# Residual updates in batches of rows through SBUF, and the weighting of the quantile sums moved behind the next step's products

## The chip, the core and the metric

The kernel runs on one core of a Trainium2 chip. Its engines each work through a queue of their own, in order: TensorE (PE in the profile, with PEld for its weight loads), VectorE (DVE), ScalarE (ACT), GpSimd (POOL), and SyncE (SP), whose queue issues the transfers. Semaphores connect them. The metric is the time of one execution on the device, in microseconds. The kernel before takes 12865.49 us, the median of three runs (12863.24, 12865.49 and 12865.96).

## What is computed

The input is `x` (16 graphs of 1024 nodes with 64 features) and a dense 0/1 adjacency matrix per graph. Four layers follow each other, each with a residual:

```
h = relu(layernorm(x)); x = x + L0(h, adj)   # thinned adjacency, weighted quantiles, two-layer MLP
h = relu(layernorm(x)); x = x + L1(h, adj)   # ((adj + I) @ h) / rowsum, NaN replaced by 0
h = relu(layernorm(x)); x = x + L2(h, adj)   # attention of 8 heads, adjacency as a bias
h = relu(layernorm(x)); x = x + L3(h, adj)   # adj @ (h @ W) + b
```

Layer 0 is the unusual one. For each node and each feature it takes the quartiles 0.25, 0.5 and 0.75 over the values of the node's neighbours, each interpolated between two ranks, and sums them with weights 0.25, 0.5 and 0.25. So there are NQ = 6 rank queries (two for each of three quantiles).

## The kernel before

The kernel is written in a framework with tile pools. A pool has a tag and a number of buffers; a new tile of a tag takes a buffer that an older tile has left, and waits if there is none. The framework orders the instructions of each engine when the kernel is built, by their place in the program, by what they depend on and by free buffers. The resulting order of each engine's queue is fixed in the program that runs.

Two streams are woven together. The first is layer 0 (`picks`): 1536 steps, one for each graph (16), group of 8 features (8), half of the nodes (2) and query q (6). Step n runs `compare(n)`: DVE makes `le` (is the count below the rank), `wa` and `wb` (its products with two tables); PE folds `wb` and `wa` into the PSUM tile `prep` and `le` into `val`; ACT copies them out into `wi` and `vs`. In the same step come `bits(n-1)` (DVE `bit`, PE `pz`) and `value(n-2)` (DVE multiplies `vs` by a test of `pz`). After the sixth query `value` also sums the six `vs` with PE into the PSUM tile `agg`, DVE multiplies it by the weights `coef` into `w`, PE reduces `w` into `acc`, ACT copies that out, and SP writes it to a tile `z`. The `vs` tiles have a tag of their own with 8 buffers. The tables for the next six steps, the ranking of the next pair of graphs and the thinning of the next adjacency are made in the background of these steps.

The second stream is layers 1 to 3 of the graph before (`rest`). Each of its pieces yields a cost (0.3 for a block of 128 rows in layers 1 and 3, 1.0 for a block of rows and a pair of heads in layer 2), and every step of `picks` gives it 0.42 to spend. A graph has 96 steps, so 40.32 to spend, and `rest` costs 40.5. After the last step the remainder runs by itself, with more buffers (`alone`): that is what is left of graph 14 and all of graph 15.

In that stream the result of each block of rows ends in PSUM, and DVE adds it to the residual `xr` of shape [128, 8, 64] block by block:

- layer 1: row sums `rc` come out of an ACT pass over the adjacency; `weighted` makes `po` (128 x 64) in PSUM; DVE adds `h`, multiplies by 1/`rc`, tests for NaN, copies the good values into a tile that POOL has set to zero, and adds that to `xr`;
- layer 2: for each of 4 pairs of heads and 8 blocks of rows: PE scores `sp`, DVE adds the adjacency and finds the maximum (`s`, `nm`), ACT makes the exponentials with their sums, PE transposes them (`pcols`, ACT copy `eT`) and multiplies by `v` (`ao`), ACT copies (`aoT`), PE projects (`pp`, two heads of 64 columns); DVE takes the reciprocals `rs` of the sums and adds both heads to `xr` with two fused instructions;
- layer 3: `weighted` again, and DVE adds `po` to `xr`.

The tiles in PSUM share these tags: two buffers each for `pa` (`prep`, `val`, `pz`), `pc` (`px`), `pb` (`pcols`, `ao`, `pp`, `po`, `agg`, `acc` and most others) and one of twice the width for `sp`.

Of the kernel before, what the change touches and what calls it, by code (L numbers as in the profile page):

```python
# [8 lines left out]
F32 = mybir.dt.float32  # L9
BF = mybir.dt.bfloat16  # L10
# [24 lines left out]
R_TOP, R_ONE, R_MID = 32, 33, 34  # L35
# [3 lines left out]
def tile_preln_adj_stack(  # L39
# [91 lines left out]
    ident = const.tile([P, P], BF, name="ident")  # L131
    nc.vector.tensor_copy(ident, identf)
    identh = const.tile([P, P], HP, name="identh")
    nc.vector.tensor_copy(identh, identf)
# [129 lines left out]
    nc.vector.tensor_tensor(ident2, identf[:, :D], identf[:, D:], OP.add)  # L264
    ones = const.tile([P, P], BF, name="ones")
# [14 lines left out]
    shifts = const.tile([P, 6], F32, name="shifts")  # L280
# [13 lines left out]
    nc.vector.memset(shifts[:, 5:6], 1.0)  # L294

# [16 lines left out]
    sel_k = const.tile([P, NQ, P], BF, name="sel_k")  # L312
    for q in range(NQ):
        at_row(sel_q[:, q, :], ((q, -KHI), (R_TOP, ones_top * KHI), (R_MID, KHI)))
        at_row(sel_k[:, q, :], ((q, 2.0), (R_MID, -2.0), (R_ONE, 2.0)))
# [5 lines left out]
    at_row(q_add, [(q, 6.0) for q in range(1, NQ, 2)] + [(R_TOP, 8.0), (R_ONE, 8.0), (R_MID, 3.0)])  # L321
# [212 lines left out]
    def ranks(V):  # L534
# [58 lines left out]
        for n in range(len(steps) - 1, -1, -1):  # L593
# [17 lines left out]
            nc.tensor.transpose(pt[:, j, :], R[:, j * P : (j + 1) * P], identh) for j in range(C)  # L611
# [7 lines left out]
    def positions(valid):  # L619

        m1 = sb.tile([P, N], I16, tag="m1", bufs=1, name="m1")
        for t in range(NH):
            pm = pa("pm")
            adjoining(
                nc.tensor.matmul(pm, ones, valid[t][:, j, :], start=j == 0, stop=j == C - 1)
                for j in range(C)  # L630
            )
            nc.vector.tensor_scalar(m1[:, t * 512 : (t + 1) * 512], pm, -1.0, None, op0=OP.add)
            if t < NH - 1:
                yield None
        n6 = a2("n6", (P, N), I16)
        nc.vector.tensor_scalar(n6, m1, q_tau, q_add, op0=OP.mult, op1=OP.add)
        nc.vector.tensor_scalar(n6, n6, 3, None, op0=OP.logical_shift_right)
        kq = sb.tile([P, N], HP, tag="kq", bufs=2, name="kq")
        nc.scalar.copy(kq, n6)
        yield kq  # L640
        krow = []
        for q in range(NQ):

            krow.append(sb.tile([P, N], I16, tag="krow", bufs=NQ, name="krow"))
            for t in range(NH):
                hs = slice(t * 512, (t + 1) * 512)
                pk = pb("pkr")
                nc.tensor.matmul(pk, sel_k[:, q, :], kq[:, hs], start=True, stop=True)
                nc.scalar.copy(krow[q][:, hs], pk)
            if q < NQ - 1:  # L650
                yield None
        yield krow
        nr = a2("nr", (P, N), I16)
        nc.vector.tensor_scalar(nr, m1, r_tau, None, op0=OP.mult)
        nc.vector.tensor_scalar(nr, nr, 3, None, op0=OP.bitwise_and)
        coef = sb.tile([P, N], BF, tag="coef", bufs=1, name="coef")
        nc.vector.tensor_scalar(coef, nr, w_frac, w_one, op0=OP.mult, op1=OP.add)
        yield coef
# [112 lines left out]
    def picks():  # L771
# [8 lines left out]
        weights, tables, state, vs_of, els = {}, {}, {}, {}, {}  # L780
# [24 lines left out]
        def compare(n):  # L805
# [9 lines left out]
            nc.vector.tensor_tensor(wb, le, c1, OP.mult)  # L815
# [24 lines left out]
            vs = sb.tile([P, 512], F32, tag="v", bufs=8, name="vs")  # L840
# [15 lines left out]
        def value(n):  # L856
            b, g, t, q = steps[n]
            el = els[b]
            pz, vs = state.pop(n)
            nc.vector.scalar_tensor_tensor(vs, pz, 97.0, vs, op0=OP.is_equal, op1=OP.mult)  # L860
            vs_of[q] = vs
            if q < NQ - 1:
                return
            agg = pb("agg")
            adjoining(
                nc.tensor.matmul(  # L866
                    agg[32 * (q_ % 4) : 32 * (q_ % 4) + 32, :], sel_t[:, q_ // 4, :], vs_of[q_],
                    start=q_ < 4, stop=q_ > 1, tile_position=(0, 32 * (q_ % 4)),
                    skip_group_check=True,
                )  # L870
                for q_ in range(NQ)
            )
            hs = slice(t * 512, (t + 1) * 512)
            w = a2("w")
            nc.vector.tensor_tensor(w, agg, el.coef[:, hs], OP.mult)
            acc = pb("acc", (8, 512))
            nc.tensor.matmul(acc, sel_c, w, start=True, stop=True)
            nc.scalar.copy(w[:8, :], acc)
            nc.sync.dma_start(el.z[t * D + 8 * g : t * D + 8 * g + 8, t, :], w[:8, :])
# [15 lines left out]
        for n in range(last + 2):  # L895
# [21 lines left out]
            if 0 <= n - 2:  # L917
                value(n - 2)
                if (n - 1) % per == 0:
                    leave(els.pop(steps[n - 2][0]))  # L920
                    for _ in stages:
                        pass
# [151 lines left out]
    def layer1(b, xr, adjT_d):  # L1074
        h = b2_("h1", (P, C, D))
        norm_relu(xr, h, b2_)
        yield 0.5
        for i in range(C):
            ad = adj_rows(b, i)

            rc = small("rc1", [P, 1], bufs=2)
            act(ad, ad, AF.Copy, accum_out=rc)
            nc.vector.tensor_scalar(rc, rc, 1.0, None, op0=OP.add)
            nc.vector.reciprocal(rc, rc)
            aT = chunk_cols(ad, "aT1")
            nc.sync.dma_start(adjT_d[i], aT)
            po = weighted(aT, h)
            o = small("o1", [P, D], bufs=2)
            nc.vector.tensor_tensor(o, po, h[:, i, :], OP.add)
            nc.vector.tensor_scalar(o, o, rc, None, op0=OP.mult)  # L1090

            ok = small("ok1", [P, D], I32, bufs=2)
            nc.vector.tensor_tensor(ok, o, o, OP.is_equal)
            z = small("z1", [P, D], bufs=1)
            nc.gpsimd.memset(z, 0.0)
            nc.vector.copy_predicated(z, ok, o)
            nc.vector.tensor_tensor(xr[:, i, :], xr[:, i, :], z, OP.add)
            yield 0.3

    def layer2(b, xr):  # L1100
# [17 lines left out]
        HW = H * D  # L1118
        for pr in range(H // 2):

# [29 lines left out]
            for i in range(C):  # L1150
                ad = adj_rows(b, i)
                act(ad, ad, AF.Copy, scale=gm[:, i, 1:2])
                sums = small("sums", [P, 2])
# [3 lines left out]
                for t in range(NH):  # L1157
# [13 lines left out]
                    for e in range(2):  # L1171
# [6 lines left out]
                        nms[e] = nm  # L1178
                for e in range(2):
                    act(ss[e], ss[e], AF.Exp, bias=nms[e], scale=-1.0, accum_out=sums[:, e : e + 1])  # L1180
# [9 lines left out]
                rs = small("rs", [P, 2])  # L1190
                nc.vector.reciprocal(rs, sums)
# [4 lines left out]
                for e in range(2):  # L1196
                    nc.vector.scalar_tensor_tensor(
                        xr[:, i, :], pp[:, e, :], rs[:, e : e + 1], xr[:, i, :], op0=OP.mult, op1=OP.add
                    )
                yield 1.0  # L1200

    def layer3(b, xr, adjT_d):
# [10 lines left out]
        yield 0.5  # L1213
        for i in range(C):
            aT = sb.tile([P, C, P], F32, tag="bt", bufs=2, name="aT3")
            nc.sync.dma_start(aT, adjT_d[i])
            po = weighted(aT, hid)
            nc.vector.tensor_tensor(xr[:, i, :], xr[:, i, :], po, OP.add)
            yield 0.3
        nc.sync.dma_start(out[b].rearrange("(c p) d -> p c d", p=P), xr)  # L1220
# [60 lines left out]
```

## Time and profile before

The profiled execution took 12858.39 us; its span from the first to the last instruction is 12856.6 us, so 1.8 us lie around it.

| engine | busy us | share of the span | instructions |
|---|---|---|---|
| PE | 11601.9 | 90% | 86209 |
| DVE | 11662.2 | 91% | 21644 |
| ACT | 9453.7 | 74% | 16250 |
| POOL | 24.5 | 0% | 138 |

The mean granted clock of TensorE is 0.986. Three stages can be told apart in time. The first step of `picks` starts at 350 us; before that DVE ranks the first pair of graphs (PE is busy for 45 of these 350 us). The steps run until the last `le` at 12458 us. From about 12484 us to the end the last graph's layers run alone. A share of busy time is a mean over these stages. "Idle before" in a group of instructions is the time for which the engine did nothing just ahead of them, and the arrow names what it waited for.

### The profile page before, as it was taken

The numbers are of one execution on the slowest core, as the hardware profiler recorded it, in microseconds if no ns is written. First come the engines' busy times: TensorE is split into PE (matmuls) and PEld (weight loads), VectorE is DVE, ScalarE is ACT, GpSimd is POOL, SyncE is SP. The second block draws the span as 40 slices with busy tenths as digits, with TensorE's granted clock in tenths as the row PEclk, the third lists the DMA queues.
The fourth block names the chain that finished last, engine by engine and source line by source line (L and its number), as shares of the span: only waits on it lengthen the run. The fifth ranks groups of instructions, "written<-read, shape, count | busy, mean of one in ns | idle before, by whom it ended". The sixth has DMA issues, their size and how long they took to land. (4 is left out here: it accounts for less than half of the span.)

```text
span 12856.6 us, 221392 instructions
## 1 busy us (share of the span) xinstructions
PE 11601.9 (90%) x86209; PEld 5418.0 (42%) x86209; DVE 11662.2 (91%) x21644; ACT 9453.7 (74%) x16250; POOL 24.5 (0%) x138
## 2 busy tenths in 40 slices
PE   0789999999999998999999999999999999999998
PEld 0224444444444444444444444444444444444445
DVE  8999999999998999989899998999989999887873
ACT  0557777777777787777777777777777777787766
POOL 0000000000000000000000000000000000000000
PEclk9999999999999999999999999999999999999999
DMA  3012121221212122121221212122121221212012
GB/s 104 29 40 70 53 90 53 83 66 58 81 53 87 55 64 77 56 87 56 69 67 60 86 54 84 53 62 83 50 87 54 72 73 56 93 31 66 29 61 67
DMA packets 503198, 841.36 MB, mean 65 GB/s; under 512 B 238720, under 2 KB 273664, under 8 KB 502144
## 3 DMA queue, kind: packets, MB, share of 16 engines
q1 hardware_dynamic: 502144, 827.20, 20.7%
q8 instruction: 675, 11.06, 0.4%
q14 instruction: 379, 3.10, 0.1%
HBM read 616.27 MB, written 206.57 MB: 64 GB/s over the span
## 5 line engine op out<-in xcount | busy, mean ns | idle before, releaser
L813 DVE TENSOR_TENSOR wa<-le,c 128x2048 f16<-128x2048 f16 x1536 | 1879.9, 1224 | 161.7 <-PE prep L832 136.4
L727 PE MATMUL px<-valid,cw 128*128 128x512 fp8e4 x8192 | 1979.6, 382 | 0.0
L811 DVE TENSOR_TENSOR le<-cum,krow 128x2048 f16<-128x2048 int16 x1536 | 1878.3, 1223 | 17.3 <-PE val L832 15.2
L815 DVE TENSOR_TENSOR wb<-le,c 128x2048 f16<-128x2048 f16 x1536 | 1878.6, 1223 | 1.2 <-PE prep L832 1.2
L398 ACT ACTIVATE c<-px,shifts 128x512 f16<-128x512 f32 x2048 | 1414.9, 696 | 381.6 <-PE px L748 197.7
L398 ACT ACTIVATE wi<-prep,shifts 128x512 f32<-128x512 f32 x1536 | 1066.6, 694 | 491.2 <-PE prep L832 343.8
L398 ACT ACTIVATE s<-s,nm 128x1024 f32<-128x1024 f32 x1024 | 1167.6, 1142 | 243.7 <-DVE nm L1174 235.9
L727 PEld LDWEIGHTS <-cw 128*128 128x128 f16 x8192 | 801.1, 98 | 1081.1 <-issue 193.4
L1165 PE MATMUL sp<-kT,qT 64*128 64x512 f32 x4096 | 1163.1, 642 | 90.8 <-DVE nm L1174 86.5
L398 ACT ACTIVATE high<-px,shifts 128x512 f16<-128x512 f32 x1024 | 713.8, 697 | 688.1 <-PE px L727 686.8
L451 PE MATMUL pcols<-identf,s 128*128 128x128 f32 x8192 | 1132.8, 281 | 91.6 <-ACT s L398 40.9
L860 DVE SCALAR_TENSOR_TENSOR vs<-pz,vs 128x512 f32<-128x512 f32 x1536 | 1059.5, 690 | 113.6 <-PE pz L853 105.9
L451 PEld LDWEIGHTS pcols<-identf,s 128*128 128x128 f32 x8192 | 889.6, 141 | 597.2 <-ACT eT L454 270.2
L832 PE MATMUL val<-le,tab 128*32 128x512 f16 x12288 | 1112.7, 385 | 20.4 <-DVE vs L860 11.9
L454 ACT COPY eT<-pcols 128x512 f32<-128x512 f32 x2048 | 1105.6, 598 | 17.7 <-PE pcols L451 16.0
L1184 PE MATMUL ao<-eT,v 128*64 128x128 f32 x16384 | 1075.0, 276 | 41.2 <-ACT eT L454 37.9
L398 ACT ACTIVATE vs<-val 128x512 f32<-128x512 f32 x1536 | 926.4, 603 | 185.7 <-PE val L832 108.5
L1184 PEld LDWEIGHTS ao<-eT,v 128*64 128x64 f32 x16384 | 904.3, 137 | 326.5 <-ACT eT L454 249.3
L1174 DVE CUSTOM_DVE_ANT_0 s<-sp,ad,nm 128x512 f32<-128x512 f32 x1024 | 732.5, 751 | 75.7 <-PE sp L1165 75.0
L398 ACT ACTIVATE low<-px,shifts 128x512 f16<-128x512 f32 x1024 | 706.8, 696 | 81.5 <-PE px L739 80.1
L1174 DVE CUSTOM_DVE_ANT_0 s<-sp,ad 128x512 f32<-128x512 f32 x1024 | 686.2, 691 | 85.2 <-PE sp L1165 57.9
L832 PE MATMUL prep<-wb,sel_w 128*32 128x512 f16 x6144 | 639.8, 393 | 134.3 <-DVE wb L815 130.9
(263 smaller groups left out, 19090.6 us busy)
## 6 DMA issues: line engine op xcount, KB each, us to landing
ad<-in_adj_dram SPq DMA_DIRECT2D x768, 512.0 KB
adjT_d<-aT SPq DMA_DIRECT2D x128, 512.0 KB
aT<-adjT_d SPq DMA_DIRECT2D x128, 512.0 KB
md<-sm SPq DMA_DIRECT2D x216, 256.0 KB
sb<-md SPq DMA_DIRECT2D x216, 256.0 KB
rem_d<-rem SPq DMA_DIRECT2D x128, 256.0 KB
left_d<-nb SPq DMA_DIRECT2D x128, 256.0 KB
lr<-left_d SPq DMA_DIRECT2D x256, 128.0 KB
```

The source lines that it names most:

```text
L398: nc.scalar.activation(out_, in_, func, **kw)
L451: nc.tensor.transpose(pt[:, c, :], ad[:, (4 * s + c) * P : (4 * s + c + 1) * P], identf)
L454: nc.scalar.copy(aT[:, 4 * s : 4 * s + 4, :], pt)
L727: yield nc.tensor.matmul(px[pp], w[:, j, :], valid[:, j, :], start=False, stop=j == C - 1, skip_group_check=True,)
L811: nc.vector.tensor_tensor(le, cum, bc(el.krow[q][:, None, hs], [P, 4, 512]), OP.is_lt)
L813: nc.vector.tensor_tensor(wa, le, c0, OP.mult)
L815: nc.vector.tensor_tensor(wb, le, c1, OP.mult)
L832: yield nc.tensor.matmul(dst[32 * pp : 32 * pp + 32, :], w[pp], r[pp], start=i == 2, stop=i in (1, 3), tile_position=(0, 32 * pp), skip_gr ...
L860: nc.vector.scalar_tensor_tensor(vs, pz, 97.0, vs, op0=OP.is_equal, op1=OP.mult)
L1165: nc.tensor.matmul(sps[e], qT[e * D : (e + 1) * D, i * P : (i + 1) * P], kT[e * D : (e + 1) * D, hs], start=True, stop=True,)
L1174: nc.vector.tensor_tensor_reduce(ss[e][:, hs], sps[e], ad[:, hs], -1.0, 3.0e38 if t == 0 else nms[e], op0=OP.add, op1=OP.min, accum_out=nm,)
L1184: nc.tensor.matmul(ao[e * D : (e + 1) * D, :], v[:, j, e * D : (e + 1) * D], eTs[e][:, j, :], start=j == 0, stop=j == C - 1, tile_position ...
```

## The change

Layers 1 to 3 no longer update `xr` block by block from PSUM. ACT copies each block's result into an SBUF tile (`o1` and `o3` of 128 x 512, one buffer; `att` of 128 x 4 x 2 x 64, one buffer). DVE then works on the whole tile: in layers 1 and 3 once per graph, in layer 2 once for every four blocks of rows, and there only after the maxima of the block that follows. The NaN test becomes `not_equal`, with the zero copied over the bad values from a constant, so that POOL has no more tiles to clear. Layer 1 gets an additional `yield 0.2`.

In `picks` the part of `value` behind `agg` becomes a function `weigh`, which is called in the next step's `compare` and put behind its `wb` on DVE.

Three edits make room in SBUF: one identity matrix instead of two, the matrices `sel_k` left out (ACT makes `krow` from the `sel_q` product, with a scale and a bias), and 7 buffers instead of 8 for `vs`.

```diff
-    ident = const.tile([P, P], BF, name="ident")
+    ident = const.tile([P, P], HP, name="ident")
...
-    identh = const.tile([P, P], HP, name="identh")
-    nc.vector.tensor_copy(identh, identf)
...
+    none = const.tile([P, 1], F32, name="none")
+    nc.vector.memset(none, 0.0)
...
-        at_row(sel_k[:, q, :], ((q, 2.0), (R_MID, -2.0), (R_ONE, 2.0)))
...
-                nc.tensor.matmul(pk, sel_k[:, q, :], kq[:, hs], start=True, stop=True)
-                nc.scalar.copy(krow[q][:, hs], pk)
+                nc.tensor.matmul(pk, sel_q[:, q, :], kq[:, hs], start=True, stop=True)
+                act(krow[q][:, hs], pk, AF.Identity, scale=-2.0 / KHI, bias=shifts[:, 6:7])
...
-            nc.vector.tensor_tensor(wb, le, c1, OP.mult)
+            last = nc.vector.tensor_tensor(wb, le, c1, OP.mult)
+            while owing:
+                owing.pop()(last)
...
-            vs = sb.tile([P, 512], F32, tag="v", bufs=8, name="vs")
+            vs = sb.tile([P, 512], F32, tag="v", bufs=7, name="vs")
...
-            hs = slice(t * 512, (t + 1) * 512)
-            w = a2("w")
-            nc.vector.tensor_tensor(w, agg, el.coef[:, hs], OP.mult)
-            acc = pb("acc", (8, 512))
-            nc.tensor.matmul(acc, sel_c, w, start=True, stop=True)
-            nc.scalar.copy(w[:8, :], acc)
-            nc.sync.dma_start(el.z[t * D + 8 * g : t * D + 8 * g + 8, t, :], w[:8, :])
+            def weigh(behind):
+                hs = slice(t * 512, (t + 1) * 512)
+                w = a2("w")
+                with tc.issue_after(behind.ins) if behind else ExitStack():
+                    nc.vector.tensor_tensor(w, agg, el.coef[:, hs], OP.mult)
+                acc = pb("acc", (8, 512))
+                nc.tensor.matmul(acc, sel_c, w, start=True, stop=True)
+                nc.scalar.copy(w[:8, :], acc)
+                nc.sync.dma_start(el.z[t * D + 8 * g : t * D + 8 * g + 8, t, :], w[:8, :])
+
+            owing.append(weigh)
...
+        o = sb.tile([P, C, D], F32, tag="po", bufs=1, name="o1")
+        rc = small("rc1", [P, C], bufs=2)
         for i in range(C):
             ad = adj_rows(b, i)
-
-            rc = small("rc1", [P, 1], bufs=2)
-            act(ad, ad, AF.Copy, accum_out=rc)
-            nc.vector.tensor_scalar(rc, rc, 1.0, None, op0=OP.add)
-            nc.vector.reciprocal(rc, rc)
+            act(ad, ad, AF.Copy, accum_out=rc[:, i : i + 1])
             aT = chunk_cols(ad, "aT1")
             nc.sync.dma_start(adjT_d[i], aT)
-            po = weighted(aT, h)
-            o = small("o1", [P, D], bufs=2)
-            nc.vector.tensor_tensor(o, po, h[:, i, :], OP.add)
-            nc.vector.tensor_scalar(o, o, rc, None, op0=OP.mult)
-
-            ok = small("ok1", [P, D], I32, bufs=2)
-            nc.vector.tensor_tensor(ok, o, o, OP.is_equal)
-            z = small("z1", [P, D], bufs=1)
-            nc.gpsimd.memset(z, 0.0)
-            nc.vector.copy_predicated(z, ok, o)
-            nc.vector.tensor_tensor(xr[:, i, :], xr[:, i, :], z, OP.add)
+            nc.scalar.copy(o[:, i, :], weighted(aT, h))
             yield 0.3
+        nc.vector.tensor_scalar(rc, rc, 1.0, None, op0=OP.add)
+        nc.vector.reciprocal(rc, rc)
+        nc.vector.tensor_tensor(o, o, h, OP.add)
+        nc.vector.tensor_tensor(o, o, bc(rc[:, :, None], [P, C, D]), OP.mult)
+        bad = b2_("bad", (P, C, D), I32)
+        nc.vector.tensor_tensor(bad, o, o, OP.not_equal)
+        nc.vector.copy_predicated(o, bad, bc(none[:, :, None], [P, C, D]))
+        nc.vector.tensor_tensor(xr, xr, o, OP.add)
+        yield 0.2
...
+            def residual(i, att, sums):
+                rows = xr[:, i : i + C // 2, :]
+                rs = small("rs", [P, C // 2, 2], bufs=1)
+                nc.vector.reciprocal(rs, sums)
+                nc.vector.tensor_tensor(
+                    att, att, bc(rs[:, :, :, None], [P, C // 2, 2, D]), OP.mult
+                )
+                for e in range(2):
+                    nc.vector.tensor_tensor(rows, rows, att[:, :, e, :], OP.add)
...
+                while late:
+                    residual(*late.pop())
                 for e in range(2):
-                    act(ss[e], ss[e], AF.Exp, bias=nms[e], scale=-1.0, accum_out=sums[:, e : e + 1])
+                    act(ss[e], ss[e], AF.Exp, bias=nms[e], scale=-1.0, accum_out=sums[:, i % (C // 2), e : e + 1])
...
-                rs = small("rs", [P, 2])
-                nc.vector.reciprocal(rs, sums)
...
-                for e in range(2):
-                    nc.vector.scalar_tensor_tensor(
-                        xr[:, i, :], pp[:, e, :], rs[:, e : e + 1], xr[:, i, :], op0=OP.mult, op1=OP.add
-                    )
+                nc.scalar.copy(att[:, i % (C // 2)], pp)
+                if (i + 1) % (C // 2) == 0:
+                    late.append((i + 1 - C // 2, att, sums))
                 yield 1.0
+        residual(*late.pop())
...
+        o = sb.tile([P, C, D], F32, tag="po", bufs=1, name="o3")
         for i in range(C):
...
-            po = weighted(aT, hid)
-            nc.vector.tensor_tensor(xr[:, i, :], xr[:, i, :], po, OP.add)
+            nc.scalar.copy(o[:, i, :], weighted(aT, hid))
             yield 0.3
+        nc.vector.tensor_tensor(xr, xr, o, OP.add)
```

More of the change, by code (lines that the diff above doesn't have):

```diff
@@ L34 @@
 FIRST = 127.0
-R_TOP, R_ONE, R_MID = 32, 33, 34
+R_TOP, R_MID = 32, 34
 @with_exitstack
@@ L279, in tile_preln_adj_stack @@
     nc.vector.tensor_scalar(off[:, 1:2], bkt, 0.0, None, op0=OP.is_equal)
-    shifts = const.tile([P, 6], F32, name="shifts")
+    shifts = const.tile([P, 7], F32, name="shifts")
     nc.vector.tensor_scalar(
@@ L294, in tile_preln_adj_stack @@
     nc.vector.memset(shifts[:, 5:6], 1.0)
+    nc.vector.memset(shifts[:, 6:7], 2.0 * (160.0 - FIRST) + 2.0)
     def at_row(dst, terms):
@@ L311, in tile_preln_adj_stack @@
     sel_q = const.tile([P, NQ, P], BF, name="sel_q")
-    sel_k = const.tile([P, NQ, P], BF, name="sel_k")
     for q in range(NQ):
         at_row(sel_q[:, q, :], ((q, -KHI), (R_TOP, ones_top * KHI), (R_MID, KHI)))
-        at_row(sel_k[:, q, :], ((q, 2.0), (R_MID, -2.0), (R_ONE, 2.0)))
     mid_w = const.tile([P, P], BF, name="mid_w")
@@ L320, in tile_preln_adj_stack @@
     q_add = const.tile([P, 1], F32, name="q_add")
-    at_row(q_add, [(q, 6.0) for q in range(1, NQ, 2)] + [(R_TOP, 8.0), (R_ONE, 8.0), (R_MID, 3.0)])
+    at_row(q_add, [(q, 6.0) for q in range(1, NQ, 2)] + [(R_TOP, 8.0), (R_MID, 3.0)])
     r_tau = const.tile([P, 1], F32, name="r_tau")
@@ L610, in ranks @@
         adjoining(
-            nc.tensor.transpose(pt[:, j, :], R[:, j * P : (j + 1) * P], identh) for j in range(C)
+            nc.tensor.transpose(pt[:, j, :], R[:, j * P : (j + 1) * P], ident) for j in range(C)
         )
@@ L779, in picks @@
         ]
-        weights, tables, state, vs_of, els = {}, {}, {}, {}, {}
+        weights, tables, state, vs_of, els, owing = {}, {}, {}, {}, {}, []
         def make(el, g, t):
@@ L919, in picks @@
                 if (n - 1) % per == 0:
+                    while owing:
+                        owing.pop()(None)
                     leave(els.pop(steps[n - 2][0]))
@@ L1118, in layer2 @@
         HW = H * D
+        late = []
         for pr in range(H // 2):
+            def residual(i, att, sums):
[7 more added lines that the diff above has]
+                    nc.vector.tensor_tensor(rows, rows, att[:, :, e, :], OP.add)
             if alone and pr % 2:
@@ L1150, in layer2 @@
             for i in range(C):
+                if i % (C // 2) == 0:
+                    att = sb.tile([P, C // 2, 2, D], F32, tag="att", bufs=1, name="att")
+                    sums = small("sums", [P, C // 2, 2], bufs=2)
                 ad = adj_rows(b, i)
                 act(ad, ad, AF.Copy, scale=gm[:, i, 1:2])
-                sums = small("sums", [P, 2])
                 eTs = []
```

## The prediction

> **What bounds the kernel now.** The first view is the page's busy times: PE 90% and DVE 91% of the span, ACT 74%, POOL nothing. Two engines are nearly full, so neither share alone says what a microsecond on DVE is worth. For that I read the chain of waits.
>
> ```profile
> PE 21%; DVE 19%; ACT 7%; issue 2%; DMA 0%; SPq 0%; ACTq 0%; DVEq 0%
> DVE wa L813 3%; PE px L727 3%; DVE wb L815 3%; DVE le L811 3%; DVE s L1174 3%; PE ao L1184 2%; ACT s L398 2%; PE pcols L451 2%; PE sp L1165 1%; DVE vs L860 1%; PE prep L832 1%; PE val L832 1%; PE agg L866 1%; DVE bit L847 1%; ACT eT L454 1%
> ```
>
> The chain adds up to only half of the span because its earliest piece is at 6518.65 us. Over that second half DVE has 0.19 x 12856.6 = 2443 us on the chain, of 5565 us busy by the windows view of this stretch: 0.44. ACT has 7%, 900 of 4791 us: 0.19. So I count a microsecond of work taken off DVE as 0.44 on the end, and one put on ACT as 0.19. That is a rate for small shifts, not a law.
>
> Then the groups that the change touches, with the idle time ahead of them:
>
> ```profile
> L1197 DVE SCALAR_TENSOR_TENSOR xr<-pp,rs,xr 128x64 f32<-128x64 f32 x1024 | 291.0, 284 | 137.4 <-PE pp L1195 132.9
> L875 DVE TENSOR_TENSOR w<-agg,coef 128x512 f32<-128x512 f32 x256 | 177.0, 691 | 100.7 <-PE agg L866 67.4 <-PE pz L852 31.9
> L1191 DVE RECIPROCAL rs<-sums 128x2 f32<-128x2 f32 x512 | 84.7, 165 | 84.4 <-ACT s L398 80.5
> L1089 DVE TENSOR_TENSOR o<-po,h 128x64 f32<-128x64 f32 x128 | 28.6, 223 | 66.2 <-PE po L1071 64.8
> L1218 DVE TENSOR_TENSOR xr<-xr,po 128x64 f32<-128x64 f32 x128 | 27.9, 219 | 90.6 <-PE po L1071 90.1
> L1083 DVE TENSOR_SCALAR rc<-rc 128x1 f32<-128x1 f32 x128 | 18.7, 150 | 33.3 <-ACT ad L398 33.1
> ```
>
> The reader is to see that DVE, the busiest engine, stands for 512.6 us ahead of these short instructions, out of about 1194 us that it is idle at all. Each is the end of a chain through PE and ACT, sits in DVE's queue at a fixed place, and holds up `le`, `wa` and `wb` behind it.
>
> Last, the timeline of DVE, because durations overlap:
>
> ```profile
> 12451.09 0.16 DVE L1191 RECIPROCAL rs<-sums 128x2 f32<-128x2 f32 x1
> 12451.17 1.21 DVE L811 TENSOR_TENSOR le<-cum,krow 128x2048 f16<-128x2048 int16 x1
> 12452.29 0.69 DVE L860 SCALAR_TENSOR_TENSOR vs<-pz,vs 128x512 f32<-128x512 f32 x1
> 12452.89 0.68 DVE L1174 CUSTOM_DVE_ANT_0 s<-sp,ad 128x512 f32<-128x512 f32 x1
> ...
> 12456.77 0.29 DVE L1197 SCALAR_TENSOR_TENSOR xr<-pp,rs,xr 128x64 f32<-128x64 f32 x1
> 12456.96 0.69 DVE L860 SCALAR_TENSOR_TENSOR vs<-pz,vs 128x512 f32<-128x512 f32 x1
> ```
>
> The next instruction starts 0.08 to 0.09 us before the last one ends. An instruction so takes its duration less 0.09: the reciprocal 0.08, an `xr` update 0.19, a 512-wide one 0.60.
>
> **The change, part by part.** The sum is made against 12858.39 us.
>
> *DVE's work.* Layer 2 removes 512 x (0.08 + 2 x 0.19) = 236 us. It adds 128 batches: a reciprocal of 8 columns (0.20 by L424, so 0.11), a 512-wide product (0.60) and two 256-wide sums. No row has that width; between 0.13 (64 wide, 0.22 less 0.09) and 0.60 (512 wide) a line through the element counts gives 0.33, and 128 x 1.37 = 175 us (124 to 244 at the ends). Layer 1 removes seven instructions a block, 0.15, 0.16, 0.22, 0.25, 0.22, 0.23 and 0.22 us, less 7 x 0.09: 128 x 0.82 = 105 us; it adds per graph two small ones (0.17) and five 512-wide ones: 16 x 3.17 = 51 us. `not_equal` and the predicated copy are not in the trace at this width; at 64 they cost what an addition does, so I take an addition's row. Layer 3 goes from 128 x 0.13 = 17 to 16 x 0.60 = 10 us. Together -61 - 54 - 7 = -122 us, times 0.44: **-54** (ends -106 to +1, from the two widths and no effect). `w` keeps its 256 x 0.69.
>
> *DVE's waits.* The new instructions read SBUF tiles that ACT filled, in layer 2 a whole block of rows later, so the 512.6 us have no cause at these places. At the rate of 0.44 they are 226 us. Not all comes back: DVE arrives earlier at `wa`, which already waits 161.7 us, 136.4 of it for PE's `prep`. I take two thirds, **-150** (ends 0 and -226). The weakest share is `w`: in the built order of the changed program it stands on average 15.7 DVE instructions behind the last `vs` product of its group, before 15.9. Only its short distances are gone (the second tenth goes from 7 to 9.4). Its `acc`, ACT copy and SP transfer go with it; SP already stands 1191.8 us at that transfer for ACT, and the adjacency loads queued behind it run three buffers ahead (ACT waits 33.7 us for them at L398's `ad` in layer 2), so I cost that at nothing; without that cover it would be these 34 us.
>
> *ACT's work.* 512 copies of `pp`, like L1193 (same shape, 0.291): 149 us. 256 of `po`, between L398's accumulator read of one column (0.209) and L1069 (128 wide, 0.267): 0.24, 61 us (54 to 68). `krow` takes a bias, so L398's 0.696 in place of L649's 0.596: 192 x 0.10 = 19 us. The built order has 42 table loads in place of 34; in the timeline each pushes its neighbours 1.31 us apart: 10 us. Together 239 us x 0.19 = **+45** (ends 0 and +239).
>
> The Trainium skill, page "ScalarE: Activation LUTs", section "What ACT_TABLE_LOAD costs", gives about 2.66 us for a switch with its drain, where the trace shows 1.31; by the page the eight loads would be an estimated 21 us, and the term +47. Its section "Rules for kernel authors" speaks against the change: additions and the like belong on VectorE, which is faster per element. What that rule leaves out is which queue is full, and the chain's shares are about that.
>
> *ACT's waits.* Each new copy stands right behind a PE product of its own block, as `aoT` does. Those wait 148.5 us (L1193, 512 of them) and 158.7 us (L1069, 256), 307 us together. The new ones wait for one short product (`pp`, 0.48 us) where `aoT` waits for 16 or 32, so I take half, 154 x 0.19 = **+29** (ends 0 and +307). Queued behind are `wi`, `vs` and the `px` copies, which PE waits for.
>
> *Seven `vs` buffers.* With eight, the copy `vs<-val` of a group's third step takes the buffer that the group's `agg` has to read first; with seven it is the second step. The trace has this wait already: "ACT vs L398 <- PE agg L866: 67.3, 51". In the built order this copy now stands 7.8 ACT instructions behind its `wi`, before 1.6, so `val` keeps one of two `pa` banks meanwhile. Pairing `agg` with `val` step by step through the timeline, I find `agg` ending after the third step's `val` in 92 of 255 groups; holding `prep` until then would push it by 548 us in all. The ends are 0 and 548 x 0.44 = 241; since a freed bank before `agg` lets other work run, I take half of the nearest row, **+34**.
>
> *The rest.* 19 pairs of constant instructions and six matrices leave the start, at about 0.13 us each pair beside other work: **-3** (0 to -8). `rest` now costs 40.7 a graph against 40.32: over 15 graphs the overhang grows from 2.7 to 5.7, three more units run behind the last step. A block alone takes (12810 - 12567) / 31 = 7.8 us, and 3 x 7.8 = 23 are added where as much PE work leaves the steps; less overlap, and three longer ends of layers, make **+10** (0 to +30). POOL's 128 clears hid under DVE: nothing.
>
> Sum: -54 - 150 + 45 + 29 + 34 - 3 + 10 = -89, so 12769 us on the profiled execution. The median stands 7.1 us above it: **12776 us**, -0.7%.
>
> **The rivals.**
>
> *No change.* PE is the bound and the freed waits return at `wa<-prep`: of the 150 only 61 stay, and the sum is 0: 12865 us. For it: PE is busy for 365 to 380 us of most stretches of 400. Against it: 130.9 us of PE's own idle time ahead of `prep<-wb` and 88.6 ahead of `pz<-bit` wait for DVE.
>
> *Slower by the bank.* The late `vs` copy keeps `val`'s bank, `prep` and `pz` share the other, and DVE starves at `wa` and `vs`. At its full 241 in place of 34 the sum is +118: 12984 us. It decides from 34 + 89 = 123 us on, that is 123 / 0.44 / 92 = 3.0 us in each late group, out of at most 6. For it: the two banks and the order; against it: the 67.3 us that the same wait costs now.
>
> *Slower by ACT.* If ACT's copies weigh as much as DVE's work did, 0.44 x (239 + 154) = 173 replaces 74: sum +10, 12875 us; with all 307 of waits +77, 12943 us.
>
> **How the numbers follow.** A difference counts from 0.2%, 26 us, about what a measurement of this kernel tells from none. Forecast 0.56, no change 0.14, the bank 0.20, ACT 0.10. The forecast's own range is 12585 (DVE work at its end, waits at theirs, no new waits: -106 - 226 + 45 - 3 + 10 = -280) to 12840. Across the cases, 12560 to 12990: lower than the forecast's end because the 0.44 may be too small where DVE alone is full, and up to the bank's 12984. Faster 0.57, within 0.2% 0.12, slower 0.31.
>
> **What would show it.** Right: DVE's idle time ahead of the new batches near zero, DVE busy down by about 120 us, PE's share up, more steps per 1000 us in layers 1 and 3. Wrong: `vs<-val` waiting for `agg` far above 67 us; idle ahead of `wa` and `vs L860` grown by what left the updates; ACT's `att` copy waiting for `pp` as long as DVE did. The prediction fails if the built order, which no row of before prices, makes other products late.

## The result, and the profile after

The changed kernel takes 12743.22 us, the median of four runs (12737.83 to 12749.5), against 12864.36 for the kernel before (12861.37 to 12865.96). The ratio is 0.9904 with a 95% interval of 0.9892 to 0.9917: 121 us less. The forecast was 89 less, with the same sign. The profiled execution took 12739.76 us with a mean granted clock of 0.987.

The page's busy times and its chain of waits, for the kernel after:

```profile
PE 11508.7 (90%) x86209; PEld 5414.4 (43%) x86209; DVE 11510.5 (90%) x19675; ACT 9625.0 (76%) x17026; POOL 1.4 (0%) x10
...
DVE 29%; PE 28%; ACT 10%; issue 5%; DMA 1%; SPq 0%; DVEq 0%; ACTq 0%
```

DVE works 151.7 us less and ACT 171.3 us more, where 122 and 239 were forecast. The shares of busy time are nearly what they were, and the chain covers another part of the span than the chain of the kernel before, so neither tells where the time came from. The windows view, cut at the three stages, tells more. Its columns are the stretch, its length, and for each engine the busy time with the number of instructions. First the kernel before, then the kernel after:

```profile
0.00:350.00 350.00, 44.89 (x187) 19.63 (x188) 287.56 (x842) 50.76 (x77) 1.50 (x11) 0.98 0.32 95
350.00:12459.00 12109.00, 11216.00 (x83389) 5167.22 (x83389) 11219.03 (x20311) 9165.43 (x15741) 21.95 (x120) 0.99 0.21 64
12459.00:12856.00 397.00, 341.03 (x2639) 231.11 (x2635) 155.60 (x493) 237.47 (x433) 1.06 (x7) 0.89 0.27 84
```

```profile
0.00:347.00 347.00, 45.21 (x187) 19.77 (x188) 284.29 (x793) 52.33 (x78) 1.35 (x10) 0.98 0.31 96
347.00:12308.00 11961.00, 11098.85 (x83194) 5145.97 (x83193) 11080.40 (x18491) 9306.43 (x16422) 0.00 (x0) 0.99 0.20 65
12308.00:12738.00 430.00, 364.66 (x2830) 248.65 (x2828) 145.85 (x393) 266.22 (x528) 0.00 (x0) 0.89 0.25 82
```

The start is 3 us shorter, the steps 148, and what runs alone at the end is 33 longer. In the steps DVE (the third pair of numbers) is busy for 139 us less. It is idle there for 12109 - 11219 = 890 us before and 11961 - 11080 = 881 after. So by DVE's own account the steps lost work and kept nearly all of their idle time. PE's account (the first pair) adds up as well: with the same 86209 instructions in the whole kernel it is busy for 117 us less in the steps (the ends of its products are modelled). Such an account says what fits, not what caused it.

The groups view of the kernel after, with the instructions that took the place of the updates, and `w`:

```profile
L1130 DVE TENSOR_TENSOR att<-att,rs 128x512 f32<-128x512 f32 x128 | 88.2, 689 | 78.2 <-ACT att L1213 78.2
L1237 DVE TENSOR_TENSOR xr<-xr,o 128x512 f32<-128x512 f32 x16 | 11.0, 690 | 60.9 <-ACT o L1235 60.9
L1129 DVE RECIPROCAL rs<-sums 128x8 f32<-128x8 f32 x128 | 25.8, 202 | 29.7 <-ACT s L397 29.3
L1096 DVE TENSOR_TENSOR o<-o,h 128x512 f32<-128x512 f32 x16 | 11.0, 688 | 26.4 <-ACT o L1092 26.3
L1134 DVE TENSOR_TENSOR xr<-xr,att 128x256 f32<-128x256 f32 x256 | 108.3, 423 | 1.9
L878 DVE TENSOR_TENSOR w<-agg,coef 128x512 f32<-128x512 f32 x256 | 176.4, 689 | 90.8 <-PE agg L867 88.5 <-PE val L833 1.1
```

The 512.6 us of idle time ahead of the touched instructions are 288 here. Counting only what lies in the steps (from the timeline), 354 became 152: 201 us went. The other 159 us of the 512.6 were never in the steps. They lay where the last graph runs alone, and there DVE is idle for 241 of 397 us anyway.

Most of those 201 us came back. The untouched groups with the longest waits, before and then after:

```profile
L813 DVE TENSOR_TENSOR wa<-le,c 128x2048 f16<-128x2048 f16 x1536 | 1879.9, 1224 | 161.7 <-PE prep L832 136.4 <-ACT c L398 12.3 <-ACT eT L454 6.1
L860 DVE SCALAR_TENSOR_TENSOR vs<-pz,vs 128x512 f32<-128x512 f32 x1536 | 1059.5, 690 | 113.6 <-PE pz L853 105.9 <-ACT vs L398 6.0
L1174 DVE CUSTOM_DVE_ANT_0 s<-sp,ad,nm 128x512 f32<-128x512 f32 x1024 | 732.5, 751 | 75.7 <-PE sp L1165 75.0
L1174 DVE CUSTOM_DVE_ANT_0 s<-sp,ad 128x512 f32<-128x512 f32 x1024 | 686.2, 691 | 85.2 <-PE sp L1165 57.9 <-PE pcols L451 20.7 <-PE pv L1144 2.7
```

```profile
L812 DVE TENSOR_TENSOR wa<-le,c 128x2048 f16<-128x2048 f16 x1536 | 1878.1, 1223 | 250.2 <-PE prep L833 190.0 <-PE val L833 24.3 <-ACT c L397 19.3
L861 DVE SCALAR_TENSOR_TENSOR vs<-pz,vs 128x512 f32<-128x512 f32 x1536 | 1057.8, 689 | 161.1 <-PE pz L854 140.1 <-ACT w L881 5.4 <-ACT ad L397 4.8
L1191 DVE CUSTOM_DVE_ANT_0 s<-sp,ad,nm 128x512 f32<-128x512 f32 x1024 | 728.4, 750 | 112.0 <-PE sp L1182 111.5
L1191 DVE CUSTOM_DVE_ANT_0 s<-sp,ad 128x512 f32<-128x512 f32 x1024 | 681.6, 689 | 141.7 <-PE sp L1182 105.4 <-PE pcols L450 28.6 <-ACT high L397 2.6
```

In the steps alone `wa` waits 88 us longer, the `vs` product 50 and both forms of `s` together 39: 177 of the 201. The reading is that DVE no longer stands at the updates, arrives earlier at the next instruction with a late input from PE, and stands there.

Two lines of the waits view of the kernel after (in total, times, longest) belong to what the prediction feared:

```profile
ACT att L1213 <- PE pp L1212: 130.9, 172, 1.9
...
ACT vs L397 <- PE agg L867: 59.4, 107, 1.7
```

ACT now waits for `pp` as long as DVE did (130.9 us against 132.9). The `vs` copy waits for `agg` twice as often as before, but for 59.4 us in place of 67.3.

### The profile page after: what moved, and what is told of

It reads as the page before. It is cut to its first block, busy times and chain, and to the rows that moved or that the text cites. A ratio compares the mean times of both kernels' runs of the same rounds, so it can differ in the third digit from the quotient of the medians.

```text
span 12738.0 us, 220547 instructions
## 1 busy us (share of the span) xinstructions
PE 11508.7 (90%) x86209; PEld 5414.4 (43%) x86209; DVE 11510.5 (90%) x19675; ACT 9625.0 (76%) x17026; POOL 1.4 (0%) x10
## 4 chain that ended last, share of the span: by engine, by line
DVE 29%; PE 28%; ACT 10%; issue 5%; DMA 1%; SPq 0%; DVEq 0%; ACTq 0%
DVE wa L812 5%; PE px L726 4%; DVE wb L814 4%; DVE le L810 4%; DVE s L1191 4%; PE ao L1203 3%; PE pcols L450 2%; ACT s L397 2%; DVE vs L861 2%; PE sp L1182 2%; PE prep L833 2%; PE val L833 2%; DVE bit L848 2%; PE agg L867 1%; PE two L1069 1%
```

## The experiments

Each kernel is compared with the kernel before, run beside it on the same chip. A ratio's interval is 11 to 21 us to either side, so a difference between two kernels counts from about 25 us. "Against the change" below means the difference of the two ratios, times 12864.

**Single parts put on the kernel before.** First the seven buffers alone:

```diff
-            vs = sb.tile([P, 512], F32, tag="v", bufs=8, name="vs")
+            vs = sb.tile([P, 512], F32, tag="v", bufs=7, name="vs")
```

> The kernel before with 7 instead of 8 buffers for vs, nothing else. My theory (the bank held until agg has read the buffer costs something, 34 us in the sum): 12880 to 12930 us, ACT's vs copy waiting for agg more often than 51 times, idle ahead of wa and of the vs product up by some tens of us. Rival 'slower by the bank': 12985 us or more. Rival 'it is hidden': within 26 us of 12864.

Measured: 12843.38 us, ratio 0.9982 (0.9972 to 0.9991), 23 us faster. In the waits view of this kernel:

```profile
ACT vs L398 <- PE agg L866: 127.2, 137, 2.2
```

The wait that the prediction priced at +34 did grow, from 67.3 us, and `agg` ends behind the first of the third step's `val` products in 2 groups, before in 92 (behind the last of them in none, before in 66). All the same the kernel is faster. The wait was seen rightly; that it costs time was wrong. The idle time ahead of `wa` and of the `vs` product, to which it was to pass on, went from 161.7 to 164.2 us and from 113.6 to 106.3.

The weighting one step later alone, with eight buffers:

```diff
-            nc.vector.tensor_tensor(wb, le, c1, OP.mult)
+            last = nc.vector.tensor_tensor(wb, le, c1, OP.mult)
+            while owing:
+                owing.pop()(last)
...
+            owing.append(weigh)
```

> The kernel before with only the weighting of the quantile sums called one step later, vs with 8 buffers, residuals as before. My theory gives w a share of 100.7 of the 512.6 us of waits: 100.7 x 0.44 x 2/3 = 30 us, so 12835 us, idle ahead of w down from 100.7. Rival 'w does not really move, its mean place is the same': 12864 within 26 us and idle ahead of w unchanged. A third way: agg holds its bank longer and the transposes of layer 2 wait: slower by 20 us or more.

Measured: 12848.41 us, 0.9985 (0.9976 to 0.9994), 18 us faster. The idle time ahead of `w` falls from 100.7 to 76.1 us; what was behind `pz` is gone.

Layers 1 and 3 alone in batches, with the additional `yield 0.2`, the edits that make room and seven buffers. From the changed kernel, `weigh(None)` is called at once and layer 2 is the old one:

```diff
-            owing.append(weigh)
+            weigh(None)
...
-                nc.scalar.copy(att[:, i % (C // 2)], pp)
...
+                for e in range(2):
+                    nc.vector.scalar_tensor_tensor(
+                        xr[:, i, :], pp[:, e, :], rs[:, e : e + 1], xr[:, i, :], op0=OP.mult, op1=OP.add
+                    )
```

> The changed kernel with layer 2 and the weighting as before: layers 1 and 3 in batches, with the room-making edits and 7 buffers of vs. My theory: of the sum, work 61 x 0.44 = 27 and waits (66.2 + 90.6 + 33.3) x 0.44 x 2/3 = 56 off, the cost of the buffers and of ACT's 256 copies and new waits about 34 + 25 on: 12840 us. Rival 'the whole gain is layers 1 and 3, since their stretches take 8.9 us a step against 7.7': 12760 us. Rival 'none of it is there': 12890 or more.

Measured: 12784.91 us, 0.9935 (0.992 to 0.995), 82 us faster: more than the expected 12840, less than the rival's 12760.

Layer 2 alone in batches, with seven buffers and the room, and without the `yield 0.2`:

```diff
-            owing.append(weigh)
+            weigh(None)
...
-            nc.scalar.copy(o[:, i, :], weighted(aT, h))
+            po = weighted(aT, h)
...
+            nc.vector.tensor_tensor(xr[:, i, :], xr[:, i, :], z, OP.add)
             yield 0.3
...
-        yield 0.2
```

> The changed kernel with layers 1 and 3 and the weighting as before: layer 2 in batches, with the room-making edits and 7 buffers of vs. My theory: work 61 x 0.44 = 27 and waits (137.4 + 84.4) x 0.44 x 2/3 = 65 off, buffers 34 and ACT's 512 copies and new waits about 45 on: 12850 us. Rival 'the whole gain is layer 2': 12760 us. Rival 'ACT takes back what DVE gives': 12890 or more.

Measured: 12808.27 us, 0.9954 (0.9939 to 0.9969), 59 us faster, again between what was expected and the rival. Seven buffers stand in both of the last two, so the single parts can't be added up: 82 + 59 + 18 is more than the whole.

**One part taken back from the changed kernel.** The weighting at once, which is the first line pair of the diff above by itself:

> The changed kernel with the weighting in its old place, all else as changed. By itself on the kernel before the move gave 0.15%. If the parts add up: 12743 + 18 = 12761 us, idle ahead of w back from 91 to about 100 or more. Rival 'with the residuals out of DVE's way the move is worth nothing': 12743 within 15 us. Rival 'the move pays only in the new order': 12780 or more.

Measured: 12781.81 us, 0.9939 (0.9925 to 0.9954), 45 us slower than the change. The groups view of this kernel has

```profile
L878 DVE TENSOR_TENSOR w<-agg,coef 128x512 f32<-128x512 f32 x256 | 175.6, 686 | 130.2 <-PE agg L867 88.7 <-PE pz L853 39.3 <-PE val L833 0.4
```

The later place takes away 39.3 us behind `pz`. The 88.7 behind `agg` are the same with it and without it. Without it DVE's idle time in the steps is 916 us, 35 more than in the changed kernel, with the same work.

Eight buffers, with `att` in the tag "po" so that they fit; and a second kernel with that tag and seven buffers:

```diff
-            vs = sb.tile([P, 512], F32, tag="v", bufs=7, name="vs")
+            vs = sb.tile([P, 512], F32, tag="v", bufs=8, name="vs")
...
-                    att = sb.tile([P, C // 2, 2, D], F32, tag="att", bufs=1, name="att")
+                    att = sb.tile([P, C // 2, 2, D], F32, tag="po", bufs=1, name="att")
```

> The changed kernel with 8 buffers of vs; att shares the buffer of o1 and o3 to make room for it. My prediction held the seventh buffer's loss for a cost; on the kernel before it was a gain of 0.18%. If that gain is there in the changed kernel too: 12743 + 23 = 12766 us, agg again ending after the third step's val in many groups (2 now, 92 before). If the cost of the prediction is there after all: 12710 us. If the order is all chance: anywhere within 25 us of 12743, with no relation to where agg ends.

> The changed kernel with att sharing the buffer of o1 and o3, vs with 7 buffers: the same as the run with 8 buffers but for the one buffer. Theory 'seven buffers bring a little in the changed kernel too': 10 to 23 us faster than that run's 12752. Rival 'it is sharing the buffer that cost those 9 us': 12752, and the eighth buffer is worth nothing.

Measured: 12751.67 us, 0.9916 (0.9902 to 0.9931) with eight; 12749.61 us, 0.9909 (0.9895 to 0.9922) with seven. The tag costs 6 us and the eighth buffer another 9, neither of which can be told from nothing. In the changed kernel no effect of the number of buffers can be seen.

Layer 2's update with its old instructions block by block, but on the SBUF tile and at the late place, so that only DVE's work comes back:

```diff
-                nc.vector.reciprocal(rs, sums)
...
+                for k in range(C // 2):
+                    nc.vector.reciprocal(rs[:, k, :], sums[:, k, :])
+                    for e in range(2):
+                        nc.vector.scalar_tensor_tensor(
+                            rows[:, k, :], att[:, k, e, :], rs[:, k, e : e + 1], rows[:, k, :],
+                            op0=OP.mult, op1=OP.add,
+                        )
```

> The changed kernel, but in layer 2 DVE runs the old instructions (a reciprocal and two fused updates for each block of rows) on the SBUF copies, at the same late place: the waits are gone as in the change, the work is as before. If the waits are what pays, as in my sum (65 of 92 us in layer 2): 12743 + 27 = 12770 us. Rival 'the work is what pays': layer 2's own gain of about 36 us is gone, 12780 us or more with DVE busy up by 61 us. Rival 'neither': 12743 within 10 us.

Measured: 12761.61 us, 0.9924 (0.9907 to 0.994). DVE works 60 us more, and the time is 26 us longer: about 0.4 for a microsecond, with an uncertainty as large as itself. In the steps DVE is busy for 52 us more and idle for 32 less.

The same for layers 1 and 3: the old seven instructions for each block, behind the loop, on the SBUF tile:

```diff
+        for i in range(C):
...
+            nc.vector.tensor_tensor(o[:, i, :], o[:, i, :], h[:, i, :], OP.add)
...
+            nc.vector.tensor_tensor(xr[:, i, :], xr[:, i, :], o[:, i, :], OP.add)
         yield 0.2
...
-        nc.vector.tensor_tensor(xr, xr, o, OP.add)
+        for i in range(C):
+            nc.vector.tensor_tensor(xr[:, i, :], xr[:, i, :], o[:, i, :], OP.add)
```

> The changed kernel, but in layers 1 and 3 DVE runs the instructions block by block (seven for each block in layer 1, one in layer 3) on the SBUF copies, after the last block: no waits in the loop, the work as before. If the waits pay: 12743 + 27 = 12770 us or less, the stretches between two layers 2 at 8.5 to 8.6 us a step. Rival 'the work pays': the gain of layers 1 and 3, about 59 us, is gone: 12800 us or more and about 8.9 us a step there.

Measured: 12751.17 us, 0.9914 (0.99 to 0.9929). DVE works 70 us more, the time is 13 us longer, which can't be told from nothing. In the steps DVE is busy for 60 us more and idle for 43 less.

These two kernels were to tell work from waits: both keep the copies and the late place and bring the old work back. The rivals in which the work pays needed 12780 and 12800 us or more, and neither came. So the shorter work accounts for some 39 of the 121 us, with an uncertainty of the same size, and the larger part of the gain stays without it. They also show that DVE's idle time in the steps is no fixed amount: it gives way when work is added.

The `yield 0.2` left out:

```diff
         nc.vector.tensor_tensor(xr, xr, o, OP.add)
-        yield 0.2
```

> The changed kernel without the additional yield 0.2 of layer 1: the layers' stream costs 40.5 a graph again, so 15 x 0.2 = 3 units fewer are left behind the last step. In the changed kernel the part behind the last le took 430 us against 397 before. My sum has +10 us net for this: 12733 us, the part behind the last step about 400 to 410 us, the steps about 20 us longer. Rival 'the steps take it for nothing': 12720 us or less. Rival 'the steps have no room': 12743 or more.

Measured: 12785.93 us, 0.9937 (0.9925 to 0.995), 42 us slower than the change. One line that issues no instruction is worth a third of the gain. The windows of this kernel's steps and end:

```profile
347.00:12385.00 12038.00, 11153.06 (x83386) 5159.24 (x83384) 11105.55 (x18517) 9323.90 (x16450) 0.00 (x0) 0.99 0.20 64
12385.00:12793.00 408.00, 339.07 (x2635) 232.09 (x2632) 135.38 (x365) 246.76 (x489) 0.00 (x0) 0.88 0.24 82
```

The end is 22 us shorter without it, as a smaller overhang should make it (23 were forecast for these three units). The steps are 77 us longer in this execution. Of these 77, 52 are idle time of DVE.

**A suspected cost doubled.** ACT copies `pp` a second time, into a tile that nobody reads:

```diff
                 nc.scalar.copy(att[:, i % (C // 2)], pp)
+                nc.scalar.copy(small("twice", [P, 2, D], bufs=1), pp)
```

> The changed kernel with a second copy of each pp by ScalarE into a tile that nobody reads: ACT has 512 copies (138 to 149 us) more to do, DVE and PE have the same. It measures what ACT's work costs the end. My rate of 0.19: 12743 + 27 = 12770 us. Rival 'ACT has slack, its copies are free': 12743 within 10 us. Rival 'ACT weighs as much as DVE', 0.44 and more: 12805 us or more.

Measured: 12744.63 us, 0.9906 (0.9891 to 0.9921). The groups view:

```profile
L1214 ACT COPY twice<-pp 128x128 f32<-128x128 f32 x512 | 145.1, 283 | 0.0
```

145 us of copies are added, ACT's busy time grows by 81 us, and the time by 3, with an uncertainty of some 25. A price of 0.44 and more, which was expected to give 12805 us or more, is excluded. Between nothing and the prediction's 0.19 (28 us for the 145, 15 for the 81) this run hardly decides; nothing is the nearer.

**Why fewer buffers help.** If `agg` ending late was what cost time with eight buffers, its products should help when they go first:

```diff
+            hi = tc.high_priority()
+            hi.__enter__()
             agg = pb("agg")
...
+            hi.__exit__(None, None, None)
```

> The kernel before, vs with 8 buffers, with the products of agg placed with high priority when the order is built. It asks why 7 buffers were faster by themselves: with them agg ended after the third step's val in 2 groups in place of 92. If the earlier agg is the reason: 12840 us as with 7 buffers, with few late groups. Rival 'the fewer buffers changed the order by chance, and agg's place means nothing': within 15 us of 12864 or elsewhere, though agg is early. Rival 'an early agg takes the bank from layer 2': slower than 12880.

Measured: 12893.84 us, 1.0019 (1.001 to 1.0027), 25 us slower. The edit didn't do what it was meant to: `agg` still ends behind the first of the third step's `val` products in 90 groups. So it says nothing on the question. It does show that the same instructions in another built order can cost 25 us.

**All of them by stretch.** Cut at the score products `sp`, the span of every kernel falls into four parts that add up to it: up to graph 0's first `sp`; layer 2, the 15 stretches from a graph's first `sp` to its last; between, the 14 gaps from there to the next graph's first, which hold layers 3 and 1 and the change of graphs; and the end behind graph 14's last `sp`. From the timelines, in us:

| kernel | `yield 0.2` | first | layer 2 | between | end |
|---|---|---|---|---|---|
| before | no | 1109 | 8845 | 2504 | 399 |
| seven buffers | no | 1107 | 8840 | 2484 | 402 |
| weighting later | no | 1107 | 8853 | 2479 | 402 |
| `agg` first | no | 1112 | 8863 | 2521 | 399 |
| layer 2 in batches | no | 1105 | 8786 | 2510 | 406 |
| change without the yield | no | 1107 | 8748 | 2529 | 407 |
| layers 1 and 3 in batches | yes | 1112 | 8835 | 2425 | 406 |
| change, weighting at once | yes | 1110 | 8836 | 2421 | 414 |
| change, eight buffers | yes | 1100 | 8826 | 2417 | 408 |
| change, `att` in the tag "po" | yes | 1099 | 8839 | 2397 | 411 |
| change, `pp` copied twice | yes | 1097 | 8840 | 2396 | 407 |
| change, layer 2 block by block | yes | 1095 | 8856 | 2401 | 406 |
| change, layers 1 and 3 block by block | yes | 1097 | 8835 | 2419 | 403 |
| change | yes | 1098 | 8839 | 2397 | 404 |

The column "between" splits by the yield: 2479 to 2529 us without it, 2396 to 2425 with it. All kernels with the yield also update layers 1 and 3 from SBUF; the one that does so without it, with 2529 us, shows that it is the yield that divides them. Layer 2 is shorter with its batches only without the yield (8845 to 8786 and 8748). With the yield these stretches take about as long as before, batches or not. By this table the changed kernel's gain lies almost wholly between: 107 of 119 us.

But the stretches don't hold the same work. Layer 0 makes its tables in the background, and the yield moves where that falls. Of ACT's 168 copies `krow` that lie in these two columns' stretches, 148 to 151 lie between in every kernel without the yield, and 86 to 88 in every kernel with it; the rest lie in layer 2. From the kernel without the yield to the changed one, PE is busy between for 2154 us in place of 2261 and in layer 2 for 8350 in place of 8262; ACT for 1799 in place of 1884 and 7063 in place of 6974. So by PE's account 107 of the 132 us by which "between" falls there are work that has moved, and layer 2 grows by 91 us. DVE's idle time falls by 96 us between and grows by 59 in layer 2. What is gained is the difference, and the columns alone don't show where it arises.

## Why the prediction came out right, and where its steps failed

The sign and the range were right. The single steps were not: errors on both sides cancelled, so that the sum came out near is in part luck. A ladder from the kernel before to the changed one shows it, each rung with the prediction's own terms:

| rung | forecast | measured |
|---|---|---|
| eight `vs` buffers to seven | +34 | -23 |
| layer 2 in batches, and the room | -27 - 65 + 28 + 14 = -50 | -36 (59 less 23) |
| layers 1 and 3 in batches, weighting later | -27 - 56 - 30 + 12 + 15 = -86 | -22 (81 less 59) |
| `yield 0.2` | +10 | -42 |

(The forecasts are the terms for DVE's work, its waits, ACT's work and its waits, split by group; the last 3 us, for the start, `krow` and the table loads, are left out.) Each rung is uncertain by some 15 to 25 us, and another order gives other rungs: taken back from the changed kernel, the weighting is worth 45, the shorter work of layer 2's batches 26, that of layers 1 and 3 13, the yield 42, and for the buffer nothing can be seen.

**DVE's work (-54).** About right. Busy time fell by 151.7 us where 122 were forecast; the 256-wide sum took 0.423 us where the line through the element counts gave 0.42, and the predicated copy 0.78 where an addition's 0.69 was taken. The rate of 0.44 lies within what the two block-by-block kernels allow, 26 us for 60 and 13 for 70, though neither fixes it: together they give 39 where the sum had 54.

**DVE's waits (-150).** This is the step that failed. "I take two thirds" of 512.6 x 0.44: 159 of the 512.6 lay at the end, where DVE is idle most of the time anyway, and while 201 us left the steps at these instructions, 177 were added at `wa`, `vs` and `s`. DVE's idle time in the steps fell by 9 us. No kernel was run that takes the waits away and nothing else, so what they are worth by themselves is not measured. The rival "no change" had named that way back (`wa<-prep`), and only its size was taken too small. That the rung of layers 1 and 3 is a quarter of its forecast agrees with it. `w` was called the weakest share, and its idle time did stay in the steps (91 to 90 us); yet taking its move back costs 45 us. The comparison with the kernel before hides what the move does: with all else changed and `w` in its old place, its idle time is 130.2 us, and the move takes it to 90.8.

**ACT's work and waits (+45, +29).** The sizes were near, as the groups view of the kernel after has them:

```profile
L1213 ACT COPY att<-pp 128x128 f32<-128x128 f32 x512 | 137.5, 268 | 134.2 <-PE pp L1212 130.9 <-DVE sd L600 0.6
L1235 ACT COPY o<-po 128x64 f32<-128x64 f32 x128 | 26.9, 210 | 34.2 <-PE po L1078 33.9
L1092 ACT COPY o<-po 128x64 f32<-128x64 f32 x128 | 26.8, 210 | 13.5 <-PE po L1078 12.5
```

That is 0.268 us for a `pp` copy (0.291 forecast), 0.21 for a `po` copy (0.24), and 182 us of waiting where 154 were forecast. ACT's busy time still grew by only 171 us, in part because the sum counted these copies at their full length and their median start is 0.09 us before the end of the instruction ahead. The price seems too high: 512 more copies cost 3 us, but that run can't exclude a small price. The waits were not taken away by themselves; that they cost nothing is inferred. The rival "slower by ACT" is excluded by the result and by that run. The rule of the Trainium skill (page "ScalarE: Activation LUTs", section "Rules for kernel authors") that additions and products belong on VectorE rather than on ScalarE is not put to the test here: what ACT was given are plain copies, and the additions and products stayed on DVE.

**Seven buffers (+34).** Wrong sign by itself (-23), and nothing that can be seen in the changed kernel. The rival "slower by the bank" counted on 241 us here; the wait it starts from is 59.4 us after. Why fewer buffers help the kernel before stays open.

**The rest (-3, +10).** The start came out right (350.0 to 346.5 us). Behind the last step 33 us were added, above its bound of 30. What was missed is that the same yield shortens the steps by more: it was booked as 0.2 more to pay for, not as a shift of one stream against the other. That it moves layer 0's table work from the stretches between graphs into layer 2 is shown by the counts behind the table; why the time falls by it is not. Layers 1 and 3 in batches without the yield were not run by themselves either, so their 82 us can't be split directly; the ladder puts most of it on the buffers and the yield. A kernel with the yield alone, on the kernel before, was not run either.

Of the signs named in advance, DVE's busy time came true, and so did more steps in layers 1 and 3 (9.04 us a step between the graphs, then 8.50), though in part because work had moved out of these stretches. DVE's idle time ahead of the new batches is not near zero: 197 us of the 288, 62 of them in the steps. PE's share stayed at 90%. Two that were to show it wrong came true as well, the longer waits at `wa` and `vs` and ACT's at `pp`, and the time fell all the same. They speak against the step, not against the sum. No version that was run beats the changed kernel; the two nearest (12744.63 and 12749.61 us) equal it.

## What to carry to other kernels

Idle time ahead of an instruction on a nearly full in-order engine is not a gain in waiting: first leave out what lies in stages where that engine is idle anyway, then ask which next instruction has a late input and will take the wait over. A share of the chain of waits is a guess at the price of work added to an engine with a quarter of its time free: add the work once more and measure. An account of busy and idle time that adds up is not yet a cause: put the work back and see whether the time comes back. Before two stretches are compared, count whether they hold the same work. Where two streams are woven by pacing constants, such a constant deserves a run of its own, since here it was worth as much as the instructions saved (42 us and some 39), and an edit that changes only the built order can move this kernel by 0.2%.

## What the runs showed of the hardware that was not expected

A table load on ACT holds it for 1.283 us, in the groups view of the kernel after:

```profile
L397 ACT ACT_TABLE_LOAD x42 | 53.9, 1283 | 29.4 <-DVE rq_f L340 28.6
```

In 33 of the 42 the next instruction starts at most 1.314 us after the end of the one before the load. The Trainium skill, page "ScalarE: Activation LUTs", section "What ACT_TABLE_LOAD costs", has about 1.28 us for the load itself, which agrees, and a drain of about 1.38 us with it, 2.66 in all. For that drain there is no room at these 33 loads, so here the price is 1.31. And ACT's copies overlap: 512 of 283 ns, each right behind the copy of the same tile (their median start is 0.105 us before its end), raised ACT's busy time by 81 us and not by 145, some 0.16 us for a copy.
